# Layer 0 of a gated two-layer block as one stream beside the attention, with contexts reloaded from DRAM

## The chip, the cores and the metric

The kernel runs on one core of a Trainium2 chip. The metric is device time in microseconds (us) of one execution; three runs of the kernel before gave 2119.4, 2120.05 and 2121.59, median 2120.05. The engines are TensorE (PE, with its weight loads PEld), VectorE (DVE), ScalarE (ACT), GpSimd (POOL), and SyncE (SP), whose queue issues the DMAs.

## The reference, cut to what matters

Four independent sequences (batches) of 512 rows and 512 columns, x, pass through two layers; each batch has a context of 512 x 256.

```
layer 0, mixer:  v = conv4(context @ in_proj); u = silu(v)          512 channels
                 dt, B, C = u @ x_proj;  delta = softplus(dt_proj(dt) + b)
                 state[n] = state[n] * exp(delta * A[n]) + delta * u * B[n]   n = 0..15, along time
                 y = sum_n state[n] * C[n] + D * u
                 x += tanh(g) * (y * silu(layernorm(x)))
layer 0, ffn:    h = silu(bitlinear(q, gate)) * bitlinear(q, val);  x += tanh(g) * bitlinear(h, out)
                 (activations quantised to 127 steps a row, weights to -1, 0, 1)
layer 1, attn:   16 heads of 128, keys and values from the context, queries from layernorm(x),
                 q and k normalised, softmax over 512;  x += tanh(g) * (attn @ Wo)
layer 1, ffn:    4 experts of 512 (expert t takes rows 4q + t); x += tanh(g) * expert(layernorm(x))
```

A batch needs its own layer 0 before its own attention; batches do not depend on each other. Work of a later batch's layer 0 can therefore stand beside an earlier batch's attention.

## The kernel before, in words

**Precision.** Attention and expert matmuls work on pairs of f16 tiles, a high and a low half (`split`, L241; `mm3`, L246: three matmuls for each product). Making such a pair of a weight ("staging", L274) reads it as f32, squares it on ACT for its norm, fixes a power of two, splits it on ACT and DVE, and stores it to DRAM in f16. A group of weights (`attention_weights`, L333) holds wq, wk and wo of four heads; there are four groups.

**Layer 0** is two generators. `scan(b)` (L500) yields 48 times: four channel blocks (in-projection on PE, convolution on DVE), four for delta, then two halves (t0 = 0 and 2) of 16 states n and 4 output pieces. A state n loads the rows B[n] and C[n], broadcast over 128 partitions, as tiles bc and cc (L589 to L592); for each of two blocks ACT makes dA, POOL h = du * bc, DVE runs the recurrence (L603) and multiplies by cc (L604; in two of eight cases POOL does), and PE transposes h into the accumulator py (L579). `bitnet(b)` (L654) yields 24 times: `hidden` (L678; four column pieces n for each of four row blocks, with matmuls pg and pv) and `project` (L717; matmuls po). Its three ternary weight tiles w3, 1 MB each, are loaded for each batch. So layer 0 of a batch is 72 steps.

**Attention** of a batch is 16 heads. The main loop (from L1214) runs over i from -2 to 63 with a pipeline of three phases: queries of head i+2 (pq), scores and softmax of head i+1 (ps, pr, hl, pT), weighted values of head i (pav), with the output projection (pwo) after every fourth head. Keys of the next group of four heads are made in between (KPOS, L1239), values when a group's first head comes to its weighted sum.

**Order.** Instructions are issued to each engine in an order that a planner makes when the kernel is built. It follows the order of the code as a priority, but lets later instructions pass those which its own timing estimates hold to be waiting. On each engine the planned order is then fixed. Every tile has a tag with a number of slots; a tile that finds no slot free waits for the release of an older one.

**Where layer 0 stands before.** In the prologue (L1137 to L1188): context 0, scan(0) beside the making of the ternary weights, context 1, bitnet(0) with its biases in two of the five `wide` slots, group 0 of the attention weights, the keys of heads 0 to 3, and the values of batch 0 (`first_values`, L363). Layer 0 of batch 1 starts 12 heads ahead of the attention that needs it, that of batches 2 and 3 16 heads ahead (LEADS); while one is at work each of the ten turns of a head (L1231) takes one of its steps (RATE_S, RATE_B of 1.0). Weight groups 1 and 2 are placed after i = -1 and 1, and group 3 in small pieces from i = 3 on (`staging_small`, L299), one or two pieces behind each half of a head's softmax (`filler`, L1129). From i = 48 on the same filler runs three batches' experts beside the last attention; the last batch's experts follow at the end (`last_experts`).

**Tiles that the change touches.** x has two slots of 1 MB (f32). The context pair cT has two slots, used for layer 0's in-projection (L510) and, in the same tile, for keys and values. inp, the in-projection's pair, stays in SBUF. Four `big` slots of 1 MB hold u, delta and du of a scan, the w3 of a bitnet, and staging. The small f32 tiles have tags (MIDS, L67): "g" 6 slots (bc, cc, g), "v" 6 (h, gv and others), "t" 4 (low, ud, zth, acc, exr). PSUM has eight banks: four of `pss` for layer 0 and four for the prologue's `psp`, later for attention.

```
for i in range(-2, n):
    ...
    for k, g in enumerate((q, s, q, s, w, s, w, s, w, q)):
        next(g, None)
        if behind:
            rate += RATE_B if in_bitnet[0] else RATE_S
            while rate >= 1 and behind:
                rate -= 1
                if next(behind[0][1], behind) is behind:
                    behind.pop(0)
```

Of the kernel before, what the change touches and what calls it, by code (L numbers as in the profile page):

```python
# [40 lines left out]
P = 128  # L41
# [25 lines left out]
MIDS = {"g": 6, "v": 6, "t": 4, "q": 2, "n": 1, "x": 1, "y": 2}  # L67
STAGE = (-1, 1)
STAGE_SMALL = {3: 3}
FILL0 = 2  # L70
RATE_S = 1.0
RATE_B = 1.0
SRB = 1
SHB = 1
EARLY = 1
# [36 lines left out]
LEADS = {1: 12, 2: 16, 3: 16}  # L112
# [4 lines left out]
def flamingo_kernel(  # L117
# [15 lines left out]
    ctxp = ctx.enter_context(tc.tile_pool(name="ctxp", bufs=2))  # L133
# [43 lines left out]
    def load_x(b):  # L177
        x_sb[b] = xpool.tile([P, T, L], F32, tag="x", name=f"x{b}", bufs=2)
        nc.sync.dma_start(x_sb[b], x[b].rearrange("(p t) f -> p t f", t=T))
# [43 lines left out]

    def total_pow2(tot, pool, name):

        n = tot.shape[1]
        ps = ap(f"frobps{name}") if pool is None else psum(pool, f"frobps{name}")
# [31 lines left out]
    def raw_load(name, src):  # L259
        raw = bigt([P, src.shape[1] * src.shape[2]], F32, f"raw{name}")  # L260
# [13 lines left out]
    def staging(name, src, n, ps_pool, raw=None, store=True):  # L274

        if raw is None:
            raw = raw_load(name, src)
        w = raw.shape[1]
        hl = bigt([P, 2 * w], F16, f"hl{name}")
        v = hl.rearrange("p (n s m) -> p n s m", n=n, s=2)  # L280
        pieces = [
            (raw[:, j * 512 : (j + 1) * 512], *(v[:, j, s] if n > 1 else v[:, 0, s, j * 512 : (j + 1) * 512] for s in range(2)))
            for j in range(w // 512)
        ]
        tot = sm(4, "stot", f"stot{name}", 2)
        for j, (r, hi, lo) in enumerate(pieces):
            nc.scalar.activation(hi, r, AF.Square, accum_out=tot[:, j : j + 1])
# [11 lines left out]
    def staging_small(name, src, n, ps_pool):  # L299

        k = src.shape[1] * src.shape[2] // 512
        m = src.shape[1] // k
        d = dram.tile([P, k * 1024], F16, name=f"d{name}")
        v = d.rearrange("p (n s m) -> p n s m", n=n, s=2)
        tot = sm(4, "stot", f"stot{name}", 2)

        def load(j):
            raw = at.tile([P, 512], F32, tag="sraw", name=f"sraw{name}{j}", bufs=SRB)
            j %= k
            nc.sync.dma_start(raw.rearrange("p (a b) -> p a b", a=m), src[:, j * m : (j + 1) * m])  # L310
            return raw

        raws = [load(j) for j in range(SRB)]
        for j in range(2 * k):
            hl = at.tile([P, 2, 512], F16, tag="shl", name=f"shl{name}{j}", bufs=SHB)
            if j < k:
                nc.scalar.activation(hl[:, 0], raws[j], AF.Square, accum_out=tot[:, j : j + 1])
            else:
                if j == k:
                    S = total_pow2(tot[:, :k], ps_pool, name)  # L320
                split(raws[j], hl[:, 0], hl[:, 1], S[:, 1:2])
                j -= k
                nc.sync.dma_start(v[:, j] if n > 1 else v[:, 0, :, j * 512 : (j + 1) * 512], hl)
                j += k
            if j + SRB < 2 * k:
                raws.append(load(j + SRB))
            yield
        return d, S, None

    def stage_attention_weights(hg, ps_pool):  # L330
        run(attention_weights(hg, ps_pool, staging))
# [31 lines left out]
    def first_values(pool, ps_tile):  # L363

        for hg in range(NG):
            raw = pool.tile([P, 2, 512], F32, tag="rv", name=f"rawv{hg}", bufs=2)
            nc.sync.dma_start(raw, Wv[:, hg * 512 : (hg + 1) * 512].rearrange("(k p) c -> p k c", p=P))
            wv = pool.tile([P, 2, 2, 512], F16, tag="wv", name=f"wv{hg}", bufs=2)
            S = frobenius(raw, wv[:, 0], psv, f"wv{hg}")
            split(raw, wv[:, 0], wv[:, 1], S[:, 1:2])  # L370
            Sv.append(S)
            wv_d.append(dram.tile([P, 2048], F16, name=f"dwv{hg}"))
            nc.sync.dma_start(wv_d[hg], wv.rearrange("p s k c -> p (s k c)"))
            for b in range(PRE):
                for c, v in enumerate(
                    values_of(b, hg, wv, ps_tile, lambda s, d, n: pool.tile(s, d, tag="v", name=f"o{n}", bufs=VB))
                ):
                    nc.sync.dma_start(v_d[b][hg][:, c, :], v.rearrange("p s c -> p (s c)"))

# [40 lines left out]
    cT = [None] * B  # L420
    Sc = [None] * B

    def context(b, raw_tile, junk_tile, ps_pool):
        cn = raw_tile([P, T, DM], F32, f"cn{b}")
# [16 lines left out]
        cT[b] = ctxp.tile([P, 2, 2, L], F16, tag="cT", name=f"cT{b}")  # L441
        split(raw, cT[b][:, 0], cT[b][:, 1], Sc[b][:, 1:2])


    context(0, bigt, bigt, pss)
    inp = const.tile([P, 2, 2, T * P], F16, name="inp")
# [3 lines left out]
    split(raw, inp[:, 0], inp[:, 1], Si[:, 1:2])  # L450
    xpr = const.tile([P, T, DR + 2 * DS], F32, name="xpr")
# [48 lines left out]
    def scan(b, of_8=DVE_OF_8, G=2, y_tile=lambda name: psum(pss, name), between=lambda n, ins: None):  # L500

        cwb = small.tile([P, T, DC], F32, tag="cwb", name=f"cwb{b}")
# [4 lines left out]
        for t in range(T):  # L507
            ps = psum(pss, f"pin{b}{t}")
            cols = slice(t * P, (t + 1) * P)
            mm3(ps, [(inp[:, 0, k, cols], inp[:, 1, k, cols], cT[b][:, 0, k], cT[b][:, 1, k]) for k in range(2)])  # L510
# [143 lines left out]
    def bitnet(b, w_tile=bigt, ps_tile=lambda name: psum(pss, name), biases=None):  # L654
# [23 lines left out]
        def hidden(t, xqT, sgv):  # L678
# [4 lines left out]
            for n in range(4):  # L683
                cols = slice(n * 512, (n + 1) * 512)
                pg = psum(pss, f"pg{nm}{n}")
# [76 lines left out]
    def attention(b):  # L762
        xt = x_sb[b]
        c_ = cT[b]
# [313 lines left out]
    def early_experts():  # L1078
# [3 lines left out]
        xT = xpool.tile([P, 2, T, L], F16, tag="x", name="exT", bufs=2)  # L1082
# [21 lines left out]
    def last_experts(pool, places):  # L1104
# [8 lines left out]
        for t in (T - 1, *range(T - 1)):  # L1113
            xT = pool.tile([P, 2, T, P], F16, tag="qT", name=f"lxT{t}", bufs=2)
            xr = x_sb[b][:, t, :]
            split_normed(xr, estats[b][t], xT, slice(0, P), f"l{t}", "q")
            its = run(gate_up_of(
                t, ws[t, 0], ws[t, 1], lambda s, k: xT[:, s, k], P, f"{t}b",
                lambda s, d, name: midt(s, d, name, "t"), lambda s, d, name: midt(s, d, name, "g"), ap,
            ))  # L1120
            run(down_of(t, (b,), ws[t, 2], its, [xr], f"{t}b", ap))
# [7 lines left out]
    def filler(ins):  # L1129

        for _ in range(FILL if atts[B - 1] else FILL0):
            with tc.issue_after(ins):
                while fill and next(fill[0], fill) is fill:
                    fill.pop(0)

    ak = ctx.enter_context(tc.tile_pool(name="ak", bufs=1))
    with tc.tile_pool(name="pro", bufs=1) as pro, tc.tile_pool(name="psp", bufs=4, space=PSUM) as psp:  # L1137
# [43 lines left out]
        context(1, wide, junk, psv)  # L1181
        run(bitnet(0, wide, lambda name: psum(psp, name, "n", 2), biases))
        for hg in range(EARLY):
            stage_attention_weights(hg, psv)
        atts[0] = step, keys = attention(0)
        steps[0] = step
        run(keys(0, lambda name: psum(psp, name, "m", 2)))
        first_values(pro, lambda name: psum(psp, name, "m", 2))  # L1188
# [12 lines left out]
    in_bitnet = [False]  # L1201
    behind, rate = [], 0.0

    def layer0(b):

        in_bitnet[0] = False
        if b >= 2:
            context(b, bigt, bigt, pss)
        yield from scan(b)
        in_bitnet[0] = True  # L1210
        yield from bitnet(b)
# [56 lines left out]
    def whole(pool, tag, bufs):  # L1268
# [7 lines left out]
        "c": halves(ctxp, "cT", 2), "p": halves(at, "pT", PT), "h": halves(at, "hl", HL),  # L1276
# [56 lines left out]
```

## Time and profile before

| what | value |
| --- | --- |
| median of three runs | 2120.05 us |
| profiled execution, whole | 2116.47 us |
| its span, first to last instruction | 2114.7 us |
| mean granted PE clock | 0.864 |
| DMA | 358.08 MB, mean 169 GB/s |
| first and last start of a pq matmul | 376.5 and 2005.7 us |
| h of layer 0, batches 0, 1, 2, 3 (first to last start) | 61.1 to 169.8, 438.1 to 621.5, 837.9 to 1018.1, 1248.5 to 1423.3 us |
| pg to po of layer 0, batches 0, 1, 2, 3 | 203.3 to 294.4, 657.7 to 765.0, 1052.4 to 1157.7, 1457.2 to 1578.9 us |

The page of a profile gives the busy time of each engine; the span in 40 slices of about 53 us, each digit the busy share in tenths (9 is 90% or more; PEclk is the clock granted to PE in tenths of full speed); and groups of instructions by line and tile. Busy times of a stretch come from a separate view whose rows are start:end, length, then each engine's busy time with its number of instructions, the mean granted clock, the DMA share and GB/s. A row for one tile gives line, engine, operation, output <- inputs, count, and least, median and longest duration in ns, then first and last start in us. A tile's name is that of the code without numbers: pq is every query matmul.

### The profile page before, as it was taken

The page shows a single profiled execution, that of the slowest core. Times are in us where ns is not written, and L with a number is a line of the kernel's source. Part 1 is how long each engine was busy: PE and PEld are TensorE (multiplying, and loading weights), DVE is VectorE, ACT ScalarE, POOL GpSimd, SP SyncE. Part 2 cuts the span into 40 slices and gives each one's busy share as a digit, 9 for nine tenths or more (in the row PEclk, how much of TensorE's full clock was granted, in tenths as well). Part 3 has the DMA queues.
Part 4 walks back from the last instruction along what each step waited for, and adds up shares of the span by engine and source line. Part 5 has one row for each costly group of instructions (what it writes and reads, how often), then busy time and mean ns, then how long its engine had stood idle before and what let it go on. Part 6 is the DMA issues. An engine that isn't in the chain of part 4 may idle for free. (4 is left out here: it accounts for less than half of the span.)

```text
span 2114.7 us, 26915 instructions
## 1 busy us (share of the span) xinstructions
PE 1619.9 (77%) x8238; PEld 905.6 (43%) x8238; DVE 1659.6 (78%) x3237; ACT 1202.2 (57%) x2575; POOL 1006.5 (48%) x914
## 2 busy tenths in 40 slices
PE   3464654777676988777898967787899879788986
PEld 1343221345443444454444434444444445445445
DVE  5798855699998987999998679998885665555753
ACT  6866355665544666564546664654465565657633
POOL 2775330276664545766536367774253431313211
PEclk8555867889888998888899988898999989899998
DMA  7454176667888866776776567767765776867753
GB/s 248 157 166 139 25 194 224 191 157 200 188 223 209 191 138 159 191 179 164 184 184 143 121 152 206 176 165 192 165 148 124 169 165 189 182 163 192 184 127 100
DMA packets 525202, 358.08 MB, mean 169 GB/s; under 512 B 424768, under 2 KB 427456, under 8 KB 519040
## 3 DMA queue, kind: packets, MB, share of 16 engines
q1 hardware_dynamic: 525056, 356.36, 66.9%
q8 instruction: 64, 1.05, 0.2%
q14 instruction: 82, 0.67, 0.1%
HBM read 214.98 MB, written 38.54 MB: 120 GB/s over the span
## 5 line engine op out<-in xcount | busy, mean ns | idle before, releaser
L186 POOL TENSOR_TENSOR h<-du,bc 128x512 f32<-128x512 f32 x256 | 333.5, 1322 | 88.1 <-PE py L579 69.5
L579 PE MATMUL py<-ident,h 128*128 128x128 f32 x1024 | 196.8, 339 | 118.8 <-DVE h L604 109.1
L596 ACT ACTIVATE dA<-delta,A 128x512 f32<-128x512 f32 x256 | 172.0, 687 | 191.5 <-DVE h L604 132.1
L902 ACT ACTIVATE pr<-ps,nmx,rqs 128x512 f32<-128x512 f32 x256 | 196.9, 774 | 124.2 <-DVE nmx L894 119.4
L603 DVE TENSOR_TENSOR_SCAN dA<-dA,h 128x512 f32<-128x512 f32 x208 | 249.3, 1216 | 11.6 <-ACT dA L596 11.3
L252 PE MATMUL ps<-kT,qT 128*128 128x512 f16 x768 | 214.4, 402 | 49.8 <-ACT pr L902 45.4
L252 PE MATMUL pq<-axnT,wq 128*128 128x512 f16 x768 | 213.5, 436 | 35.2 <-DMA axnT<-xsa 15.0
L252 PE MATMUL pav<-pT,v 128*128 128x256 f16 x1536 | 205.7, 286 | 43.6 <-DVE v L244 14.7
L579 PEld LDWEIGHTS py<-ident,h 128*128 128x128 f32 x1024 | 163.0, 213 | 161.3 <-DVE h L604 139.5
L926 DVE SCALAR_TENSOR_TENSOR hl<-pr,den,hl 128x512 f16<-128x512 f32 x214 | 195.8, 926 | 24.7 <-POOL hl L925 15.0
L252 PEld LDWEIGHTS <-v 128*128 128x128 f16 x1536 | 156.2, 103 | 99.1 <-issue 30.8
L884 DVE TENSOR_REDUCE nmx<-ps 128x1 f32<-128x512 f32 x256 | 172.7, 680 | 28.6 <-PE ps L252 27.9
L252 PE MATMUL pwo<-wo,oT 128*128 128x512 f16 x768 | 180.9, 384 | 9.9 <-DVE oT L244 5.2
L252 PEld LDWEIGHTS <-cT 128*128 128x128 f16 x768 | 83.7, 110 | 170.1 <-issue 108.8
L925 POOL TENSOR_SCALAR hl<-pr,den 128x512 f16<-128x512 f32 x86 | 64.5, 750 | 189.1 <-DVE den L912 59.7
L252 PEld LDWEIGHTS <-wq 128*128 128x128 f16 x768 | 85.0, 112 | 154.4 <-issue 92.4
L252 PE MATMUL pk<-wk,cT 128*128 128x512 f16 x384 | 119.1, 457 | 33.9 <-DVE ssq L873 11.3
L186 POOL TENSOR_TENSOR g<-g,gv 128x512 f32<-128x512 f32 x64 | 83.5, 1310 | 120.3 <-DVE gv L708 44.6
L252 PEld LDWEIGHTS <-qT 128*128 128x128 f16 x768 | 77.9, 103 | 143.7 <-issue 77.5
L604 DVE TENSOR_TENSOR h<-dA,cc 128x512 f32<-128x512 f32 x208 | 138.0, 676 | 0.6
L183 POOL TENSOR_TENSOR rqs<-ssq,mhalf 128x4 f32<-128x4 f32 x64 | 69.0, 1078 | 134.9 <-DVE ssq L873 101.5
L252 PE MATMUL pw<-wv,cT 128*128 128x512 f16 x384 | 102.5, 413 | 28.7 <-DVE ov L244 11.9
(379 smaller groups left out, 3442.0 us busy)
## 6 DMA issues: line engine op xcount, KB each, us to landing
bc<-bd SPq DMA_DIRECT2D x112, 256.0 KB, 3.9
cc<-bd SPq DMA_DIRECT2D x112, 256.0 KB, 4.3
wq<-dwq SPq DMA_DIRECT2D x64, 256.0 KB, 3.6
wo<-dwo SPq DMA_DIRECT2D x64, 256.0 KB, 4.0
w<-w3d SPq DMA_DIRECT2D x12, 1024.0 KB, 7.0
g<-in_gate_b SPq DMA_DIRECT2D x48, 256.0 KB, 3.8
gv<-in_val_b SPq DMA_DIRECT2D x48, 256.0 KB, 4.4
de<-hle SPq DMA_DIRECT2D x9, 1024.0 KB, 5.3
```

Source lines behind the costliest of these rows:

```text
L183: nc.gpsimd.tensor_tensor(res, arg, mhalf[:, : arg.shape[1]], ALU.pow)
L186: nc.gpsimd.tensor_tensor(out, a, b, ALU.mult)
L252: nc.tensor.matmul(ps, l, r, start=first and i == 0, stop=last and i == n - 1)
L579: nc.tensor.matmul(ys[g // gs][:, g % gs, t, :], src[:, g::T], ident, is_transpose=True, start=first and t == 0 and g % gs == 0, stop=last ...
L596: last = nc.scalar.activation(dA, delta[:, t0 + t, :], AF.Exp, scale=A[:, t0 + t, n : n + 1])
L603: nc.vector.tensor_tensor_scan(dA, dA, h, 0.0, ALU.mult, ALU.add)
L604: nc.vector.tensor_tensor(h, dA, cc, ALU.mult)
L884: nc.vector.tensor_reduce(nmx[:, c : c + 1], ps, AX.X, ALU.max, negate=True)
L902: mark[0] = nc.scalar.activation(pr, scs[c], AF.Exp, bias=nmx[:, one], scale=rqs[:, one], accum_out=den[:, c - c0 : c - c0 + 1],).ins
L925: nc.gpsimd.tensor_scalar(hl[:, c, 0], prs[c], den[:, one], 1.0, ALU.mult, ALU.mult)
L926: nc.vector.scalar_tensor_tensor(hl[:, c, 1], prs[c], den[:, one], hl[:, c, 0], ALU.mult, ALU.subtract)
```

## The change

Layer 0 of batches 1 to 3 becomes one stream. It begins in the prologue: batch 1's steps stand beside bitnet(0) (0.6 of a step for each of its steps), beside the attention weights (0.3), the keys (0.5) and the values (0.5), by BESIDE. In the loop a turn takes 0.4 of a step, for scan and bitnet alike; batch 2 is queued behind batch 1 at i = 0, batch 3 at i = 16. All four weight groups are staged in the prologue (EARLY 4), in `wide` slots, and the small staging goes. All contexts are made before bitnet(0) and stored to DRAM; a scan loads its own again (one slot, cTs) and an attention too (one slot, cTa). inp goes to DRAM and a scan loads it to a `big` slot. x has three slots, "t" three. Since layer 0 of batch 1 holds the banks of `pss` in the prologue, pg, keys and values use `psp` there, two banks each tag. In the last experts the tile `it` takes "v" slots.

```
-MIDS = {"g": 6, "v": 6, "t": 4, "q": 2, "n": 1, "x": 1, "y": 2}
-STAGE = (-1, 1)
-STAGE_SMALL = {3: 3}
-FILL0 = 2
-RATE_S = 1.0
-RATE_B = 1.0
...
-EARLY = 1
+MIDS = {"g": 6, "v": 6, "t": 3, "q": 2, "n": 1, "x": 1, "y": 2}
+FILL0 = 3
+RATE = 0.4
+EARLY = 4
...
-LEADS = {1: 12, 2: 16, 3: 16}
+STARTS = {2: 0, 3: 16}
+BESIDE = (0.6, 0.3, 0.5, 0.5)
...
-    ctxp = ctx.enter_context(tc.tile_pool(name="ctxp", bufs=2))
+    ctxp = ctx.enter_context(tc.tile_pool(name="ctxp", bufs=1))
...
-        x_sb[b] = xpool.tile([P, T, L], F32, tag="x", name=f"x{b}", bufs=2)
+        x_sb[b] = xpool.tile([P, T, L], F32, tag="x", name=f"x{b}", bufs=3)
...
+    def load_context(b, use):
+
+        t = ctxp.tile([P, 2, 2, L], F16, tag=f"cT{use}", name=f"cT{use}{b}")
+        nc.sync.dma_start(t.rearrange("p s k l -> p (s k l)"), cT_d[b])
+        return t
...
-        cT[b] = ctxp.tile([P, 2, 2, L], F16, tag="cT", name=f"cT{b}")
+        use = "s" if b else "a"
+        cT[b] = ctxp.tile([P, 2, 2, L], F16, tag=f"cT{use}", name=f"cT{b}")
         split(raw, cT[b][:, 0], cT[b][:, 1], Sc[b][:, 1:2])
+        if b:
+            nc.sync.dma_start(cT_d[b], cT[b].rearrange("p s k l -> p (s k l)"))
...
-    inp = const.tile([P, 2, 2, T * P], F16, name="inp")
+    inp_d = dram.tile([P, 4 * T * P], F16, name="inpd")
+    inp0 = inp = bigt([P, 2, 2, T * P], F16, "inp0")
...
+        if b == 0:
+            inp, c_ = inp0, cT[0]
+        else:
+            inp = bigt([P, 2, 2, T * P], F16, f"inp{b}")
+            nc.sync.dma_start(inp.rearrange("p s k e -> p (s k e)"), inp_d)
+            c_ = load_context(b, "s")
...
     def attention(b):
         xt = x_sb[b]
+        if b:
+            cT[b] = load_context(b, "a")
...
-        context(1, wide, junk, psv)
-        run(bitnet(0, wide, lambda name: psum(psp, name, "n", 2), biases))
+        for b in range(1, B):
+            context(b, wide, junk, psv)
+
+
+        behind.append((1, layer0(1)))
+
+        def beside(steps, pieces):
+
+            rate = 0.0
+            for _ in steps:
+                rate += pieces
+                while rate >= 1:
+                    rate -= 1
+                    next(behind[0][1], None)
...
+        beside(bitnet(0, wide, lambda name: psum(psp, name, "n", 2), biases, narrow), BESIDE[0])
...
         for hg in range(EARLY):
-            stage_attention_weights(hg, psv)
+            beside(attention_weights(hg, psp, staged), BESIDE[1])
         atts[0] = step, keys = attention(0)
         steps[0] = step
-        run(keys(0, lambda name: psum(psp, name, "m", 2)))
-        first_values(pro, lambda name: psum(psp, name, "m", 2))
+        beside(keys(0, narrow), BESIDE[2])
+        beside(first_values(pro, narrow), BESIDE[3])
...
-        for b4, lead in LEADS.items():
-            if i + 2 + lead == b4 * NH:
+        for b4, start in STARTS.items():
+            if i == start:
                 behind.append((b4, layer0(b4)))
...
-                rate += RATE_B if in_bitnet[0] else RATE_S
+                rate += RATE
...
-        if i in STAGE_SMALL:
-            fill.append(attention_weights(STAGE_SMALL[i], None, staging_small))
-        if i in STAGE:
-            for hg, j in enumerate(STAGE):
-                if j == i:
-                    stage_attention_weights(hg + EARLY, pss)
```

More of the change, by code (lines that the diff above doesn't have):

```diff
@@ L64 @@
 DVE_OF_8 = (0, 1, 2, 4, 5, 6)
-MIDS = {"g": 6, "v": 6, "t": 4, "q": 2, "n": 1, "x": 1, "y": 2}
-STAGE = (-1, 1)
-STAGE_SMALL = {3: 3}
-FILL0 = 2
-RATE_S = 1.0
-RATE_B = 1.0
-SRB = 1
-SHB = 1
-EARLY = 1
+MIDS = {"g": 6, "v": 6, "t": 3, "q": 2, "n": 1, "x": 1, "y": 2}
+FILL0 = 3
+RATE = 0.4
+EARLY = 4
 SIDE0 = 5
@@ L222, in pow2, with pool_tag @@
         return S
+    def pool_tag(pool):
+        return ("m", None) if pool is pss else ("n", 2)
     def total_pow2(tot, pool, name):
         n = tot.shape[1]
-        ps = ap(f"frobps{name}") if pool is None else psum(pool, f"frobps{name}")
+        ps = ap(f"frobps{name}") if pool is None else psum(pool, f"frobps{name}", *pool_tag(pool))
         nc.tensor.matmul(ps[:, :n], ones, tot, start=True, stop=True)
@@ L257, in flamingo_kernel, with raw_load @@
     Sq, Sk, Sv, So, ceq = [], [], [], [], []
-    def raw_load(name, src):
-        raw = bigt([P, src.shape[1] * src.shape[2]], F32, f"raw{name}")
+    def raw_load(name, src, tile=bigt):
+        raw = tile([P, src.shape[1] * src.shape[2]], F32, f"raw{name}")
         with tc.issue_after(pin[0]) if pin[0] and PINS else nullcontext():
@@ L272, in run, with staging @@
                 return e.value
-    def staging(name, src, n, ps_pool, raw=None, store=True):
+    def staging(name, src, n, ps_pool, raw=None, store=True, tile=None):
+        tile = tile or bigt
         if raw is None:
-            raw = raw_load(name, src)
+            raw = raw_load(name, src, tile)
         w = raw.shape[1]
-        hl = bigt([P, 2 * w], F16, f"hl{name}")
+        hl = tile([P, 2 * w], F16, f"hl{name}")
         v = hl.rearrange("p (n s m) -> p n s m", n=n, s=2)
@@ L297, in staging @@
         return d, S, hl
[L299 to L331, printed above, removed]
     def attention_weights(hg, ps_pool, staging):
@@ L368, in first_values @@
             wv = pool.tile([P, 2, 2, 512], F16, tag="wv", name=f"wv{hg}", bufs=2)
-            S = frobenius(raw, wv[:, 0], psv, f"wv{hg}")
+            S = frobenius(raw, wv[:, 0], psp, f"wv{hg}")
             split(raw, wv[:, 0], wv[:, 1], S[:, 1:2])
@@ L378, in first_values @@
                     nc.sync.dma_start(v_d[b][hg][:, c, :], v.rearrange("p s c -> p (s c)"))
+                    yield
     gamma_w = const.tile([P, 3], F32, name="gamma_w")
@@ L420, in flamingo_kernel @@
     cT = [None] * B
+    cT_d = [dram.tile([P, 4 * L], F16, name=f"cTd{b}") for b in range(B)]
     Sc = [None] * B
+    def load_context(b, use):
+        t = ctxp.tile([P, 2, 2, L], F16, tag=f"cT{use}", name=f"cT{use}{b}")
+        nc.sync.dma_start(t.rearrange("p s k l -> p (s k l)"), cT_d[b])
+        return t
     def context(b, raw_tile, junk_tile, ps_pool):
@@ L450, in flamingo_kernel @@
     split(raw, inp[:, 0], inp[:, 1], Si[:, 1:2])
+    nc.sync.dma_start(inp_d, inp.rearrange("p s k e -> p (s k e)"))
     xpr = const.tile([P, T, DR + 2 * DS], F32, name="xpr")
@@ L509, in scan @@
             cols = slice(t * P, (t + 1) * P)
-            mm3(ps, [(inp[:, 0, k, cols], inp[:, 1, k, cols], cT[b][:, 0, k], cT[b][:, 1, k]) for k in range(2)])
+            mm3(ps, [(inp[:, 0, k, cols], inp[:, 1, k, cols], c_[:, 0, k], c_[:, 1, k]) for k in range(2)])
             v = midt([P, L], F32, f"v{b}{t}", "v")
@@ L652, in scales, with bitnet @@
         return up, dn
-    def bitnet(b, w_tile=bigt, ps_tile=lambda name: psum(pss, name), biases=None):
+    def bitnet(b, w_tile=bigt, ps_tile=lambda name: psum(pss, name), biases=None, g_tile=lambda name: psum(pss, name)):
         xt = x_sb[b]
@@ L684, in hidden @@
                 cols = slice(n * 512, (n + 1) * 512)
-                pg = psum(pss, f"pg{nm}{n}")
+                pg = g_tile(f"pg{nm}{n}")
                 for k in range(T):
@@ L1081, in early_experts @@
         n = len(bs) * P
-        xT = xpool.tile([P, 2, T, L], F16, tag="x", name="exT", bufs=2)
+        xT = xpool.tile([P, 2, T, L], F16, tag="x", name="exT", bufs=3)
         def ps_tile(name):
@@ L1118, in last_experts @@
                 t, ws[t, 0], ws[t, 1], lambda s, k: xT[:, s, k], P, f"{t}b",
-                lambda s, d, name: midt(s, d, name, "t"), lambda s, d, name: midt(s, d, name, "g"), ap,
+                lambda s, d, name: midt(s, d, name, "v"), lambda s, d, name: midt(s, d, name, "g"), ap,
             ))
@@ L1134, in filler, with layer0 @@
                     fill.pop(0)
+    behind = []
+    def layer0(b):
+        yield from scan(b)
+        yield from bitnet(b)
     ak = ctx.enter_context(tc.tile_pool(name="ak", bufs=1))
@@ L1180, in flamingo_kernel, with narrow, staged @@
             nc.sync.dma_start(biases[-1], bias.partition_broadcast(P))
-        context(1, wide, junk, psv)
-        run(bitnet(0, wide, lambda name: psum(psp, name, "n", 2), biases))
+        for b in range(1, B):
[8 more added lines that the diff above has]
+                    next(behind[0][1], None)
+        def narrow(name):
+            return psum(psp, name, "m", 2)
+        beside(bitnet(0, wide, lambda name: psum(psp, name, "n", 2), biases, narrow), BESIDE[0])
+        def staged(*args):
+            return staging(*args, tile=wide)
         for hg in range(EARLY):
-            stage_attention_weights(hg, psv)
+            beside(attention_weights(hg, psp, staged), BESIDE[1])
         atts[0] = step, keys = attention(0)
         steps[0] = step
-        run(keys(0, lambda name: psum(psp, name, "m", 2)))
-        first_values(pro, lambda name: psum(psp, name, "m", 2))
+        beside(keys(0, narrow), BESIDE[2])
+        beside(first_values(pro, narrow), BESIDE[3])
     psa = ctx.enter_context(tc.tile_pool(name="psa", bufs=4, space=PSUM))
@@ L1199, in finish @@
         ]
[L1201 to L1211, printed above, removed]
+    rate = 0.0
     n = B * NH
@@ L1275, in flamingo_kernel @@
         "b": whole(big, "big", BIG), "x": whole(at, "xnT", 1), "k": halves(ak, "kT", KT),
-        "c": halves(ctxp, "cT", 2), "p": halves(at, "pT", PT), "h": halves(at, "hl", HL),
+        "c": lambda name: [ctxp.tile(half, F16, tag=f"cT{u}", name=name + u) for u in "as"], "p": halves(at, "pT", PT), "h": halves(at, "hl", HL),
     }
```

## The prediction

> **What bounds the kernel now.** I read the page first, then busy times of stretches, then single tiles. The page's slices say that no engine bounds the kernel all the time:
>
> ```profile
> PE 1619.9 (77%) x8238; PEld 905.6 (43%) x8238; DVE 1659.6 (78%) x3237; ACT 1202.2 (57%) x2575; POOL 1006.5 (48%) x914
> PE   3464654777676988777898967787899879788986
> DVE  5798855699998987999998679998885665555753
> PEclk8555867889888998888899988898999989899998
> ```
>
> VectorE (DVE) stands at 9 where TensorE (PE) is at 6 or 7, and falls to 5 or 6 where PE reaches 8 or 9. To put edges on this I took the first and last starts of layer 0's tiles (h and pg, po) and asked for the busy time between them:
>
> ```profile
> core 0: us, PE busy (x) PEld busy (x) DVE busy (x) ACT busy (x) POOL busy (x), PEclk, DMA share, GB/s
> 200.00:295.00 95.00, 61.64 (x214) 24.43 (x214) 73.71 (x186) 39.38 (x75) 29.22 (x28) 0.71 0.38 103
> 295.00:376.50 81.50, 37.82 (x122) 14.71 (x123) 38.25 (x93) 39.94 (x96) 17.77 (x19) 0.71 0.75 227
> 438.00:765.00 327.00, 250.96 (x1285) 146.47 (x1285) 302.84 (x552) 178.83 (x394) 199.80 (x174) 0.88 0.79 193
> 838.00:1158.00 320.00, 259.69 (x1337) 150.87 (x1336) 303.81 (x572) 173.89 (x392) 201.23 (x179) 0.90 0.71 176
> 1248.00:1579.00 331.00, 264.01 (x1334) 149.92 (x1333) 308.76 (x566) 168.51 (x363) 196.59 (x173) 0.89 0.69 171
> 1579.00:1653.00 74.00, 62.41 (x344) 33.70 (x341) 44.92 (x94) 44.72 (x126) 36.88 (x37) 1.00 0.63 132
> ```
>
> Rows three to five are layer 0 of batches 1, 2, 3 under attention heads: DVE is busy 915.4 of 978 us (0.936), PE 774.7 (0.79). The last row is attention alone: DVE 0.61, PE 0.84. The first two are the end of the prologue; in its second part DVE works 38 of 81.5 us. So the kernel alternates between stretches that DVE fills and stretches in which it idles. Up to head 48 (first pq matmul at 1653 us) DVE works 161.7 us before 200, 112.0 from there to 376.5 and 1126.4 after: 1400 of 1653. The 253 idle us are what a change of order can win.
>
> **Unit costs.** Twelve pq matmuls make a head; counting them, the pure row holds 4.4 heads. A pure head takes 74/4.4 = 16.8 us, with 14.2 of PE; for DVE I use 9.9, a little under its 10.2, since layer 0 must account for the rest. The three mixed stretches hold 32.8 heads. Layer 0 of a batch costs DVE (1126 - 48 x 9.9 - 16 of staging and contexts)/3 = 211 us, 2.93 for each of its 72 steps; and PE (774.7 - 32.8 x 14.2)/3 = 103, 1.43 a step.
>
> **The change, part by part.**
>
> *Weights (EARLY 4).* Only one group really moves:
>
> ```profile
> L287 ACT ACTIVATE hlwq<-rawwq x12: 612/613/629, 68.7 to 356.4; 128x512 f16<-128x512 f32 x12
> ```
>
> Twelve pieces are three groups of four, all squared before 356 us although the code places groups 1 and 2 in the loop: the planner had already hoisted them. The fourth moves, with twelve DVE splits less two (ten pieces at about 0.8) and its constants: 9 us of DVE, and its second reading from DRAM goes.
>
> *Contexts 2 and 3* move too: a 1.28 us DVE split each and small work, 7 us in all. They now precede bitnet(0)'s w3 loads in the same five wide slots, two of which hold biases, and share one cTs slot, so that each split waits for the previous store. One context takes from 186 (load) to 205 us; about 6 us more for each of two, so I put bitnet(0) 13 us later. Bounds: 0 (loads hoisted), 30 (wholly serial). At the start inpraw is a fifth tile for four slots and waits for cn, free at 6.2 us instead of loading at 3.7: +2.
>
> *Layer 0 of batch 1 into the prologue.* BESIDE gives 14 steps next to bitnet(0) (24 x 0.6), 5 next to each weight group (20 x 0.3, the running sum ending just under 6), 2 by the keys and 8 by the values: 44 of 72, 129 us of DVE. DVE work after 200 us becomes 112 + 9 + 7 + 129 = 257. At 0.90 busy (between scan(0)'s 1.00 and the 0.78 of bitnet(0) alone) that is 286: the first pq comes at 200 + 15 + 286 = 501 instead of 376.5.
>
> [...] The trace grants PE a clock of 0.51 from 61 to 200 us, where scan(0) runs, and 0.84 to 0.85 in the scans under attention; a py transpose takes 431 ns against 307 (950 to 1017 us). [...] So I expect the slow clock for scan(1): py occupied 60.9 us for 234, 0.26 each, against 18.1/108 = 0.17. Some 220 moved py cost PE 20 us more. By the row it is hidden: PE needs 99 + 44 x 1.43 + 20 = 182 of 286. If PE were late instead, 20 us would be lost.
>
> *Rate 0.4.* Ten turns a head give 4 steps. The remaining 28 + 72 + 72 = 172 steps last 43 heads, without a gap, since batches 2 and 3 queue up behind. DVE needs 43 x 9.9 + 172 x 2.93 = 930 us, PE 43 x 14.2 + 172 x 1.43 = 857. What share will DVE reach? Scan stretches gave 0.98, bitnet stretches (621 to 765 and its like), where PE presses too, 0.885; weighted by steps 0.94. I take 0.91, three points off, because at the old rate a backlog of layer-0 steps lay ready for DVE, and at the new one it has barely any. That gives 1022 us, 23.8 a head, with PE at 0.84, what it has in the pure row. Then 5 pure heads: 84 us.
>
> *POOL beside DVE.* DVE's hl step has a median of 742 ns in the scan of batch 1 and in pure heads, but 1214 in the scan of batch 2. [...] I take 0.
>
> *Reloaded contexts.* cTa has one slot, so batch 2's (and 3's) reload waits until the last values of the batch before have read it, with wq loads, pT transposes and bc queued behind it on SP; the keys wait for it on PE. The nearest row is a 512 KB wk load: four PE waits, 9.0 us, 2.3 each. Bounds 0 and 8 per batch; I take 2.5 for two batches, +5. Reloads of inp and cTs delay layer 0 alone; while attention has work they cost 0, without that cover 5 us each.
>
> *At no cost:* "t" from 4 to 3 (psz, zth and acc use it one after the other; at most 5 us), a third x tile (no wait on x is found; the new order needs it), two PSUM banks for pg in place of four (DVE has 73.7 us of work for the 16 passes there, 4.6 each, against a bank's hold of some 3 from pg matmul to its second use), exT and it in other slots, FILL0 (the fill queue is empty until the experts). From head 48 to the end, 462 us, nothing else changes.
>
> **Sum.** 501 + 1022 + 84 + 5 = 1612 against 1653: 41 us earlier. Span 2114.7 - 41 = 2073.7. The profiled execution took 2116.47, the median of the runs is 2120.05, 5.35 over the span: 2079 us, 1.9% less.
>
> **Rivals.** I count as the same what lies within 0.2% of 2120 (2115.8 to 2124.3), about what a measurement of this kernel can tell.
>
> *A, PE becomes the bound (slower).* Place: the 43 mixed heads. If PE does not exceed the 0.79 of the old mixed stretches, because its matmuls keep waiting for DVE results in order, they take 857/0.79 = 1085 us, 25.2 a head: head 48 at 1675, 2142 us. It decides from (1653 - 501 - 84 - 5)/43 = 24.7 us a head. For it: in no long mixed stretch does PE pass 0.81. Against it: DVE was the full engine there, and in 700 to 750 us both were (PE 48.05, DVE 48.46 of 50).
>
> *B, the prologue stays thin (about the same).* bitnet(0) and scan(1) share six g tiles, for which bitnet alone wants eight; staging reads and writes 5 MB a group next to bc and cc. With DVE at 0.78, as beside bitnet(0) now, 257 us take 330: 44 us lost, 2123.
>
> *C, better cover (faster).* DVE at 0.95 in the mixed heads and 0.93 in the prologue: 979 + 276, 53 us less than my sum, 2026. Those 50 us at 0.97 speak for it; that they are short, against.
>
> *D, the planner puts layer 0 elsewhere,* as it did with the weights. DVE's total stays, so steps slipping from prologue to loop cost or win about 10 us: inside the first case.
>
> **Numbers.** First case, with D, 2045 to 2110: 0.47. A 0.25 (0.02 of it no change), B 0.14 (0.05 faster, 0.04 same, 0.05 slower), C 0.14. Faster 0.66, same 0.06, slower 0.28. The range goes down to C's middle and up to A's, with the unknowns of contexts and reloads: 2025 to 2145.
>
> **What would show it.** First pq near 501 (490 to 545); DVE about 0.90 from 215 to there. Last po near 1520 in place of 1579; first pq of head 48 near 1612. DVE 0.91 and PE 0.84 in the mixed heads, PE clock above 0.9. From head 48, 462 us as before. It is wrong if the pace is over 24.7 us a head, if the prologue passes 545, or if the experts' stretch lengthens.

## The result, and the profile after

The changed kernel takes 2187.39 us (median of four runs, 2183.44 to 2189.9) against 2119.73: a ratio of 1.0318, 95% interval 1.0289 to 1.0347. It is slower by 3.2%, where 1.9% faster was forecast, and outside the forecast range of 2025 to 2145 us. The profiled execution has a span of 2181.4 us, 66.7 more than before.

The page of the changed kernel, the lines that answer to those shown of before (busy totals, then the slices, each 54.5 us long here):

```profile
PE 1625.4 (75%) x8238; PEld 910.1 (42%) x8238; DVE 1678.9 (77%) x3237; ACT 1196.6 (55%) x2571; POOL 1000.3 (46%) x914
PE   3453855447887777698967877898888779789876
DVE  5898799998887998889879997986654565565642
PEclk8555876559998899999977989999999899899998
```

The work is the same (DVE 19 us more, PE 6). The dip of DVE that stood in slices 6 and 7 is gone: the prologue is filled. But from slice 28 on DVE stands at 4 to 6 (2 in the last), earlier than before: layer 0 is used up. Three stretches of the changed kernel, from 200 us to the first pq, on to the last po of batch 3, and on to head 48:

```profile
core 0: us, PE busy (x) PEld busy (x) DVE busy (x) ACT busy (x) POOL busy (x), PEclk, DMA share, GB/s
200.00:549.70 349.70, 196.69 (x744) 105.82 (x745) 307.49 (x587) 183.20 (x360) 185.03 (x158) 0.69 0.65 196
549.70:1478.00 928.30, 756.12 (x3831) 415.35 (x3832) 815.67 (x1507) 509.84 (x1129) 515.99 (x462) 0.91 0.70 167
1478.00:1707.90 229.90, 186.73 (x986) 99.68 (x984) 131.83 (x279) 120.95 (x326) 83.54 (x86) 0.94 0.60 124
```

In the first row DVE is busy for 0.88, near the 0.90 expected, but with 307 us of work instead of 257, so that the first pq comes at 549.7 instead of 501. In the second neither engine is full: DVE 0.88, PE 0.81. This stretch ends after 36 heads, not 43, at 25.8 us a head (928.3/36); the third row is attention alone, some 12 heads at about 18.5 us with DVE at 0.57. Head 48 starts at 1707.9 (before 1653.2, forecast 1612), and from there the end takes 473.5 us instead of 461.5. All three signs that the prediction named for being wrong have come: a pace over 24.7 us a head, a prologue past 545, a longer stretch of experts.

The prologue's first row is not even. Where the scan of batch 1 stands beside the weight staging, from 342 to 475 us, DVE is full and PE is not:

```profile
342.00:475.00 133.00, 59.05 (x240) 43.62 (x238) 130.31 (x215) 84.06 (x194) 94.86 (x81) 0.56 0.81 250
```

### The profile page after: what moved, and what is told of

The parts are those of the page before. It is cut to its first block, busy times and chain, and to the rows that moved or that the text cites. A ratio compares the mean times of both kernels' runs of the same rounds, so it can differ in the third digit from the quotient of the medians.

```text
span 2181.4 us, 26908 instructions
## 1 busy us (share of the span) xinstructions
PE 1625.4 (75%) x8238; PEld 910.1 (42%) x8238; DVE 1678.9 (77%) x3237; ACT 1196.6 (55%) x2571; POOL 1000.3 (46%) x914
## 5 line engine op out<-in xcount | busy, mean ns | idle before, releaser
L566 PE MATMUL py<-ident,h 128*128 128x128 f32 x1024 | 209.3, 358 | 145.8 <-DVE h L591 125.9
L566 PEld LDWEIGHTS py<-ident,h 128*128 128x128 f32 x1024 | 171.5, 216 | 189.5 <-DVE h L591 156.5
L251 PE MATMUL ps<-kT,qT 128*128 128x512 f16 x768 | 207.9, 396 | 41.1 <-ACT pr L891 36.7
L251 PE MATMUL pav<-pT,v 128*128 128x256 f16 x1536 | 196.7, 282 | 37.4 <-DMA pT<-hl 15.0
L915 DVE SCALAR_TENSOR_TENSOR hl<-pr,den,hl 128x512 f16<-128x512 f32 x214 | 186.1, 884 | 31.3 <-POOL hl L914 20.2
L251 PEld LDWEIGHTS <-oT 128*128 128x128 f16 x768 | 75.3, 100 | 105.1 <-issue 12.7
L251 PEld LDWEIGHTS <-cTa 128*128 128x128 f16 x576 | 61.3, 107 | 136.7 <-issue 85.7
L912 ACT ACTIVATE hl<-pr,den 128x512 f16<-128x512 f32 x128 | 92.6, 724 | 45.6 <-DVE den L901 17.1
```

The costliest lines, as they stand in the source:

```text
L251: nc.tensor.matmul(ps, l, r, start=first and i == 0, stop=last and i == n - 1)
L566: nc.tensor.matmul(ys[g // gs][:, g % gs, t, :], src[:, g::T], ident, is_transpose=True, start=first and t == 0 and g % gs == 0, stop=last ...
L912: nc.scalar.activation(hl[:, c, 0], prs[c], AF.Copy, scale=den[:, one])
L915: nc.vector.scalar_tensor_tensor(hl[:, c, 1], prs[c], den[:, one], hl[:, c, 0], ALU.mult, ALU.subtract)
```

## The experiments

I started with three theories. Theory 1 (place): a step of layer 0 is dear in the prologue and cheap beside attention. Theory 2 (thin stream): the low rate makes the loop idle. Theory 3 (early end): layer 0 ends too soon and leaves pure heads. Theories 4 and 5 came after the runs that contradicted these; they are told where they are tested. For each run I give the first pq, the start of head 48 (heads are counted from 0), and the span. The span is that of one profiled execution; executions of the kernel before lay between 2112 and 2129 us on one chip, so a difference of a few us between two spans says little.

**Rate and place.** Four kernels on one chip; before took 2121.42 us there.

```
e2:  BESIDE = (0, 0, 0, 0); RATE = 0.5
e3:  RATE = 1.0; STARTS = {2: 14, 3: 30}
e4:  RATE = 0.36
e5 (from the kernel before):  RATE_S = RATE_B = 0.6
```

> All else as in the change, but no layer-0 step beside the prologue (BESIDE all 0) and a rate of 0.5, so that batch 1's 72 steps fit before the attention that needs them. Theory 1 (place): the loop's time is about 17 us a head plus 2.1 us a step whatever the rate, and a step in the prologue costs about 3.0 because no attention matmul stands beside it. Then the first pq comes near 395 us, the loop gains 57 steps x 2.1 = 120, and the sum is 50 us below the changed kernel: about 2137. Theory 2 (thin stream): the low rate makes the loop idle; with more thin steps in the loop the loss of the loop grows from 60 to 80 us: about 2200. Theory 3 (layer 0 ends too early, pure heads at the end): the stream ends later, fewer pure heads: about 2150.

> The changed kernel with a rate of 1.0 and starts at i = 14 and 30, the dense bursts of before; the prologue as changed. Theory 1 (place): no change of more than 10 us from 2187, since a step costs the same in the loop at any rate. Theory 2 (thin stream): dense bursts bring the loop's 60 us back: about 2125 to 2140. Theory 3 (early end): batch 3's layer 0 ends later and the last heads before 48 are no longer a long pure stretch: about 2160.

> The changed kernel with a rate of 0.36 in place of 0.40, so that the 172 nominal steps reach head 48. Theory 1 (place): 2187 within 10 us. Theory 2 (thin stream): thinner still, 2187 to 2200. Theory 3 (early end): the pure heads before 48 fall from 13 to some 8 and their idle DVE time with them: about 2160.

> The kernel before with both rates at 0.6 in place of 1.0 and nothing else: the spread alone, without the prologue. Theory 1 (place): 2120 within 10 us. Theory 2 (thin stream): slower, 2140 to 2160. Theory 3 (early end): faster by up to 20, since pure stretches between batches shrink.

| run | us | ratio to before | first pq | head 48 | span |
| --- | --- | --- | --- | --- | --- |
| e2 | 2152.7 | 1.0147 (1.0132 to 1.0162) | 515.8 | 1684.7 | 2151.0 |
| e3 | 2158.2 | 1.0173 (1.0158 to 1.0188) | 548.8 | 1685.4 | 2157.8 |
| e4 | 2152.2 | 1.0138 (1.0110 to 1.0166) | 549.7 | 1676.1 | 2149.1 |
| e5 | 2135.7 | 1.0070 (1.0055 to 1.0085) | 378.4 | 1674.2 | 2133.4 |

Three different edits land within 6 us of each other, and no theory fits all four runs. e2 was to bring the first pq to 395. It came at 515.8: the planner pulled batch 1's scan into the prologue by itself (56 of its 64 h products stand before the first pq). So BESIDE hardly decides where those steps stand. e3 (dense) and e4 (thinner) gain 29 and 35 us: dense bursts bring back half of what theory 2 wanted, and the thinner stream, which should have lost, gains as much. Theory 3 has the best numbers (2150, 2160 and 2160 for e2, e3 and e4), but not the mechanism: in e4 layer 0 ends at 1466.5, earlier than in the changed kernel (1477.5), and the loop is the shortest of all. e5 has the sign against theory 3, too: spreading alone, in the kernel before, costs 0.7%. That was theory 2's sign, in half its size.

**The same place as before.** e6 takes e3 and moves batch 1's layer 0 back to i = 2.

```
-        behind.append((1, layer0(1)))
RATE = 1.0; STARTS = {1: 2, 2: 14, 3: 30}; BESIDE = (0, 0, 0, 0)
```

> The changed kernel with layer 0 of batch 1 where it was before (queued at i = 2, BESIDE 0, rate 1.0, the others at i = 14 and 30); reloaded contexts, three x tiles and all weights in the prologue stay. It differs from the run with rate 1.0 only in the place of batch 1's layer 0. Theory 1 (a step costs about 2.9 in the prologue, 2.1 beside attention): first pq near 400, loop near 1265, tail 473: about 2140, some 20 to 35 us under the 2158 of that run. If the place costs nothing and the reloads or the slots are what costs, it stays at 2158.

It took 2179.34 us (ratio 1.0263, 1.0218 to 1.0307), 21 more than e3 where theory 1 said 20 to 35 less; again 56 h products ran before the first pq, at 518.2. Theory 1 falls as a forecast, and as a test of place the run fails, since the place did not come back.

**The end.** e1 changes one word in `last_experts`.

```
-    split_normed(xr, estats[b][t], xT, slice(0, P), f"l{t}", "q")
+    split_normed(xr, estats[b][t], xT, slice(0, P), f"l{t}", "q", "n")
```

> The changed kernel with one word more: in the last experts the normalised x takes the tag n instead of v, where the change put the four it tiles. If the end is longer by 13 us because the next expert's x finds no v slot until this expert's it tiles are released, it comes back: last pav to end 67 in place of 80 us, about 2175. If the end is longer for another reason (the two places for the contexts' memory, x slots), nothing moves: 2187.

It took 2170.33 us; the span fell by 12.9 to 2168.5. From the start of the last pav matmul to the end there are 59.3 us instead of 75.9 (62.9 in the kernel before). The rows for the f16 pair of the last experts' x (xsl, lxT), of the kernel before:

```profile
L757 POOL TENSOR_TENSOR xsl<-xnl,xsl x4: 1153/1154/1155, 2068.9 to 2075.3; 128x512 f16<-128x512 f32 x4
```

of the changed kernel, with the matmuls (peg, one for each expert) that waited for these tiles, in us and number of waits:

```profile
L744 POOL TENSOR_TENSOR xsl<-xnl,xsl x4: 1151/1152/1157, 2120.7 to 2164.5; 128x512 f16<-128x512 f32 x4
L745 SPq DMA_TRANSPOSE lxT<-xsl x4: 1232/1232/1474, 2121.8 to 2165.7; - x4
  PE peg3b L251: 9.6, 1
  PE peg0b L251: 6.8, 1
  PE peg2b L251: 3.5, 1
  PE peg1b L251: 3.2, 1
```

and of e1:

```profile
L744 POOL TENSOR_TENSOR xsl<-xnl,xsl x4: 1152/1154/1159, 2124.4 to 2134.0; 128x512 f16<-128x512 f32 x4
L745 SPq DMA_TRANSPOSE lxT<-xsl x4: 1232/1338/2097, 2125.6 to 2145.0; - x4
```

Before, the four xsl started within 6.4 us. In the changed kernel they spread over 44: each x starts only at the end of the expert before it, whose `it` tiles have the same tag (the second x at 2132.4 us, just before the last of the first expert's `it` tiles). The first expert's matmul (peg3b) waits in e1 too, 9.6 us; the waits of the other three, 13.5 us together, are gone there, and the four xsl start within 9.6 us. So the shared tag is the cause. Whether an x waits for a slot, or the planner just keeps the order of the tag, is not shown.

**Layer 0 left out.** Two kernels measure what the steps cost, and e11 does the same for the kernel before. Each ran once.

```
e9:   layer0(b) for b >= 2 only loads x
e10:  layer0(b) only loads x, b = 1, 2, 3
e11:  the same as e10, in the kernel before
```

> Leaves out layer 0 of batches 2 and 3 (their x goes into attention as loaded). Theory 1: the prologue stays at 550 us; the loop falls by 144 steps x 2.1 = 302 us from 1158, to about 855, with pure heads at 17 us. If layer 0 were hidden behind attention as the prediction held in part (DVE's share the only price), the same 144 steps cost 144 x 2.93 minus what pure heads leave idle: under 200, and the loop is above 950.

> Leaves out layer 0 of batches 1, 2 and 3. Against the run that leaves out only 2 and 3 this prices the steps beside the prologue. Theory 1: the prologue shrinks from 550 to about 395, 155 us for the 57 steps that stand before the first pq, 2.7 each or more, and the loop by the rest, about 15 steps x 2.1 = 30. If the prologue's idle time hid a good part of them, as predicted, the prologue shrinks by under 120.

> The kernel before with layer 0 of batches 1, 2 and 3 left out, the counterpart of the changed kernel's run that leaves out the same (span 1721.9, first pq 443.7). Theory 4 (the prologue's frame grew: the weight groups, staged one after the other in the wide slots that bitnet(0) holds, and the end of the prologue's memory that the attention waits for): here the first pq comes near 376, the loop takes some 820, the span 1645 to 1660; layer 0 of three batches then costs 455 to 470 in either kernel, and the change's loss is the frame's. Theory 1 (place): layer 0 is cheaper in the kernel before, the span here near 1690 to 1700.

| run | first pq | head 48 | loop between | span |
| --- | --- | --- | --- | --- |
| changed | 549.7 | 1707.9 | 1158.3 | 2181.4 |
| e9 | 561.3 | 1409.0 | 847.7 | 1874.4 |
| e10 | 443.7 | 1258.6 | 815.0 | 1721.9 |
| e11 | 378.2 | 1212.6 | 834.5 | 1669.4 |
| before | 376.5 | 1653.2 | 1276.7 | 2114.7 |

The pair e10 and e11 sorts the loss. First, e10's loop is 48 heads at 17.0 us without any layer 0; that is attention's own pace. Second, the prices: batches 2 and 3 cost (1158.3 - 847.7)/144 = 2.16 us a step in the loop. Batch 1 costs 561.3 - 443.7 = 117.6 us for the 56 steps that stand before the first pq (all 64 h and 32 of 64 pg matmuls, the same as in the changed kernel), 2.10 each (1.89 with the changed kernel's 549.7 in place of e9's 561.3). So a step costs no more in the prologue than beside attention, and theory 1, which wanted 2.7 or more there, is refuted by its own price list. The prologue's idle time did hide part of the work: the 56 steps bring 170 us of DVE work (307.49 - 137.26, see the row of e10 below) and lengthen the prologue by 106 to 118. Third, layer 0 of three batches costs 2181.4 - 1721.9 = 459.5 us in the changed kernel (2.13 a step) and 2114.7 - 1669.4 = 445.3 before (2.06 a step): the stream saved nothing. With the rates 0.36 and 0.42 it costs 427 and 428. Fourth, and against theories 1 to 3: without layer 0 of batches 1 to 3 the two kernels still differ by 52.5 us. The busy times show where. Of e10, prologue from 200 us and loop to head 48:

```profile
200.00:443.70 243.70, 104.47 (x351) 42.64 (x352) 137.26 (x363) 114.60 (x251) 57.25 (x63) 0.68 0.56 174
443.70:1258.60 814.90, 688.98 (x3648) 368.30 (x3649) 478.02 (x1036) 427.67 (x1142) 290.54 (x304) 0.94 0.62 134
```

and of e11:

```profile
200.00:378.20 178.20, 95.99 (x339) 38.51 (x340) 115.67 (x298) 82.93 (x175) 51.11 (x53) 0.74 0.54 162
378.20:1212.60 834.40, 692.48 (x3656) 370.30 (x3657) 498.48 (x1100) 448.27 (x1198) 297.51 (x310) 0.94 0.65 147
```

The columns are PE, PEld, DVE, ACT and POOL busy, clock, DMA share and GB/s. The changed prologue has 22 us more of DVE work and 32 more of ACT, but lasts 65.5 us longer, with DVE idle for 106 of 244. No engine is full there, so I looked for a longer chain of waits. The loop gives 19.5 back, and the stretch behind head 48 takes 6.5 more.

**Which chain.** Theory 4: the weight groups lost their slots (`wide`, behind bitnet(0)). Theory 5: their order: three more groups stand between bitnet(0) and the values, and attention cannot start before the prologue's memory is released.

```
e12 (from e10):     staging(*args) in place of staging(*args, tile=wide)
e13 (from e6):      the same, and x in n
e15 (from e10):     EARLY = 1; groups 1, 2, 3 after i = -1, 1, 3, in the big slots
e17 (from before):  EARLY = 4; STAGE = (); STAGE_SMALL = {}
```

> The changed kernel without layer 0 of batches 1 to 3, and with the weight groups staged in the four big slots as before, which are free here. Theory 4: the raw weights load during bitnet(0) again, the first pq moves from 443.7 to 390 to 405, the span from 1722 to about 1675. If the price of the prologue is the fourth group and the contexts themselves, it stays within 10 us of 443.7.

> The changed kernel with layer 0 placed as before (rate 1.0, starts at 2, 14, 30, BESIDE 0), weights staged in the big slots, and the last x in n; the reloaded contexts and inp, three x tiles, t of 3 and all four groups in the prologue stay. Theory 4: all three prices are taken back, 2120 to 2135. If the reloads or the slots cost something in the loop, 2150 or more.

> The changed kernel without layer 0 of batches 1 to 3 (as the run of span 1721.9 and first pq 443.7), with only weight group 0 ahead of the keys and values and groups 1 to 3 placed after i = -1, 1 and 3, in the big slots, free here. Theory 5 (order: three more groups, each about 20 us of loads and stores, stand between bitnet(0) and the values, and no attention starts before the prologue's memory is released): first pq 380 to 395, loop 825 to 840, span 1670 to 1685. If the contexts and stores cost the prologue its 65 us, first pq stays above 420.

> The kernel before with one edit: all four weight groups staged in the prologue (EARLY 4, nothing in the loop); layer 0, contexts, slots as before. Theory 5: first pq 430 to 440 in place of 376.5, loop 15 to 25 us shorter, the time 2150 to 2165. If the groups cost only their own work, as the prediction held (9 us of DVE), 2110 to 2125.

e12's first pq came at 452.3 (span 1741.5), although its first group was squared from 72.6 us on again: slots are not the cause, theory 4 falls. e13 took 2161.31 us (ratio 1.0179, 1.0134 to 1.0224), first pq 460.5: with staging slots and end as before, and the placement nearly so (14 of batch 1's h products still stand before the first pq), it stays 1.8% slower. e17 is the clean one, a single edit in the kernel before: 2144.19 us against 2118.53, ratio 1.0119 (1.0079 to 1.0158). Its rows for the queries and for the splits of wo and of the values' weights (wv):

```profile
L252 PE MATMUL pq<-axnT,wq x768: 376/379/635, 429.7 to 2032.5; 128*128 128x512 f16 x192
L243 ACT ACTIVATE hlwo<-rawwo,Swo x16: 705/706/722, 291.4 to 367.8; 128x512 f16<-128x512 f32 x16
L243 ACT ACTIVATE wv<-rawv,Swv x4: 1132/1140/1149, 368.4 to 395.4; 128x1024 f16<-128x1024 f32 x4
```

The wv are split only after the last wo group, from 368.4 on; in the kernel before the same instruction ran from 293.9 to 332.7, with the groups 1 and 2 behind it and into the first heads:

```profile
L243 ACT ACTIVATE wv<-rawv,Swv x4: 1138/1144/1151, 293.9 to 332.7; 128x1024 f16<-128x1024 f32 x4
```

So theory 5 holds in the kernel before: 53 us on the first pq for three groups, 25 won back by a shorter loop. A group takes some 20 to 25 us there (the wo splits of the four run from 291.4 to 367.8). No engine is full meanwhile, in e17:

```profile
291.00:368.00 77.00, 15.59 (x53) 8.46 (x52) 38.48 (x115) 46.39 (x127) 19.53 (x22) 0.57 0.65 213
```

e10 shows the same order in the changed frame, with wv behind the last wo split (385.7):

```profile
L242 ACT ACTIVATE wv<-rawv,Swv x4: 1134/1137/1148, 386.3 to 412.8; 128x1024 f16<-128x1024 f32 x4
```

From the other side the test does not decide. In e15 the wv splits came early again (from 324.5 on), but the planner pulled groups 1 to 3 ahead too; the first pq came at 424.5, not at the 380 to 395 of theory 5 but above the 420 that I had put down for the contexts and stores, and the span fell by 18.5 to 1703.4. For the changed frame I therefore put the price of the groups between these 18.5 us and the 30 of e17's span, as an estimate.

**The plan's own spread, and putting the gains together.**

```
e14:             RATE = 0.42
e16:             RATE = 0.42, and x in n
e18 (from e16):  context(1) before bitnet(0), contexts 2 and 3 after it
```

> The changed kernel with a rate of 0.42 in place of 0.40. If the 30 us between 0.40 and both 0.36 and 1.0 are an accident of one plan, this lands anywhere from 2150 to 2190 without order; if a thin stream of just this rate has a cause, it lies by 2187 within 8 us.

> The changed kernel with the two things that helped together: rate 0.42 and the last experts' x in n. If they add up: 2151 - 12 = 2139, still slower than before by 0.9%, since the prologue's frame stays.

> The run with rate 0.42 and x in n (2133.7 us), with contexts 2 and 3 made after bitnet(0) instead of before it. If the contexts ahead of the w3 loads hold bitnet(0) up, its first pg comes near 205 in place of 214, the first pq about 540 in place of 549, and the time falls by 5 to 12 to 2122 to 2129, level with the kernel before. If VectorE's work alone sets the prologue, nothing moves: 2133 within 5.

e14 took 2150.86 us (ratio 1.0147, 1.0122 to 1.0172). With e4 on the other side of 0.40, the changed kernel's 2187 lies some 35 us over both neighbours, with the same first pq (549.7, 549.7, 550.8) and the same end; the loss is all in the loop (1158 against 1126 and 1129). It is a property of the plan and not of the execution: e1 and e16 repeat the loops of 0.40 and 0.42 with 1159.6 and 1129.9. It stands in the mixed heads: head 36, near which layer 0 ends in all three, starts 936.6 us after the first pq at 0.40, 915.4 at 0.42 and 902.5 at 0.36. Which wait makes it I have not found. e16 took 2133.66 us, ratio 1.0067 (1.0046 to 1.0088): the two gains add up, and still do not reach the kernel before. e18 missed: bitnet(0)'s first pg came at 204.5, 9 us earlier, as expected, yet the first pq at 559.7, 10 later, and the time was 2161.67 (1.0189, 1.0175 to 1.0204). What the early contexts cost is therefore left open. Where layer 0 of the other batches is left out, the last po matmul of bitnet(0) starts at 309.3 us in e10 and at 293.7 in e11; that they hold it up fits, but is not shown. I found no version that beats the kernel before.

## Why the prediction was wrong, step by step

- **Layer 0 as DVE shares: the mis-sized term, and the largest.** My sum gives the loop 1022 + 84 = 1106 us for 48 heads and 172 steps; at attention's own 17.0 us a head that is 1.69 us a step. Measured: 2.06 before, 2.16 in the changed kernel, 1.93 and 1.95 at rates 0.36 and 0.42 (loops of 1126.3 and 1128.9 against e9). I counted DVE's idle time as free for layer 0. The kernel before, at 2.06 us for a step with 2.93 of DVE work, already hid nearly as much as any version did (at best 1.93). What attention waits for in that idle time I have not traced. With 2.06 my own sum gives 501 + 816 + 354 + 5 = 1676 for head 48, no gain at all.
- **Weights: a cost taken for nothing but its DVE work.** "Only one group really moves", I concluded from squares that all started before 356 us. The row was right and the inference wrong: groups 1 and 2 were early but off the path, beside the values and the first heads. With EARLY 4 the values wait for them. Priced at 9 us of DVE; e17 shows 53 on the first pq, less 25 in the loop, 1.2% of the time.
- **"Without a gap, 43 heads."** The planner ran layer 0 ahead: 56 steps before the first pq instead of 44. The prologue's DVE work was 307 us, not 257: the twelve steps are 35 of the 50, the rest is a frame with 137 instead of 128 and 3.04 instead of 2.93 a step. At a share near the one that I had assumed this puts the first pq 49 us late, and takes 12 x 2.06 = 25 out of the loop. How much of the 49 the order of the weights makes can't be separated, since the steps fill part of that wait. Case D, which I put at 10 us either way, was the rule; I took the rate in the code for the rate on the chip.
- **The sum again.** 1612, plus 64 for the price of a step, plus 49 for the prologue, less 25 for the steps that left the loop: 1700 for head 48, where 1707.9 was measured. The other 12 us lie behind head 48.
- **DVE share 0.91.** It was 0.88, so the direction of my three points was right and the size too small. Rival A had the sign, but not its mechanism: PE rose to 0.81, past its 0.79, and still no engine was full. Rival B is refuted: DVE was at 0.88 in the prologue.
- **"At no cost": `it` in other slots.** 12.9 us, by e1. I looked at how many slots v has and not at who holds them when: x and `it` of successive experts share them.
- **Right:** the late start of bitnet(0) (215.3 against 203.3; I said 13 + 2), the slow clock in the filled prologue (0.56 from 342 to 475 us, where a py transpose of h has a median of 421 ns, against 284 ns from 549.7 to 1478 us at a clock of 0.91), where it cost nothing that the row shows, since DVE was busy for 130 of these 133 us and PE for 59; the DVE work of a step (3.00 us over all 216, (1678.9 - 1030.4)/216 against e10; PE's was 1.60, where I had 1.43). The reload of cTa, priced at 5 us, cost PE a single wait of 0.9 us.
- **The 0 for POOL beside DVE: shown by no run.** What the traces show, from 550 to 1480 us, is a median of 747 ns and a mean of 949 for the 111 hl of DVE, before 750 and 1043 for 102.

The span's 66.7 us are thus 52.5 in the kernel without layer 0 of batches 1 to 3, and 14.2 in layer 0. Of the 52.5, the end's 13 are shown, and the weight groups make some 18 to 30 by that estimate; 10 to 21 remain, where the earlier contexts lie. The one run that moved them, e18, lost time, so this part stays open. The 14.2 belong to this one rate: at its neighbours layer 0 was 17 or 18 us cheaper than before. These 14 to 18 us are about as much as the executions of one kernel spread, and why 0.40 is the dear one stays open too.

## What to carry to other kernels

Before you price a change of order, leave out the moved work once, in both kernels: the price of one step beside the rest (2.06 us here, against 2.93 of engine time) says how much of a step is hidden already, and the frame's own length shows costs that busy shares hide. An instruction that the planner has already run early may still be off the path; what counts is whether something must wait for it once the code puts it first. Where a planner orders the instructions, judge a parameter by several neighbouring values: three rates between 0.36 and 0.42 gave 2152, 2187 and 2151 us.

## What the runs showed that I had not expected

The planner can override what the code says about order: with BESIDE at zero, and even with layer 0 queued at i = 2, 56 of 64 h products of batch 1 still ran before the first query. Only with the staging back in the big slots (e13) were they 14. Layer 0's step costs about the same (1.9 to 2.1 us) beside weight staging, where DMA and ACT work (a DMA share of 0.81 and ACT busy for 84 of 133 us from 342 to 475), as beside attention (1.9 to 2.2), where PE works (0.81 from 549.7 to 1478). And a tag shared in the last 80 us, where no engine is full (PE is busy for 37 of the last 55), cost 12.9 us, more than what separates e2, e3, e4 and e14 (7.3).
